# Graph attention over 400,000 sorted edges: the gathers of a pair of sections split into two groups of four, the first group turned half a step ahead

## The chip, the cores and the metric

The kernel runs on one core of a Trainium2 chip, as one launch. The metric is the device time of one execution in microseconds, and the figure for a kernel is the median over repeated executions. Beside the times there is one profiled execution with a trace of every engine: TensorE (PE, with its weight loads shown apart as PEld), VectorE (DVE), ScalarE (ACT), GpSimd (POOL) and SyncE (SP), which issues most of the plain transfers.

## The reference

One graph attention layer over 12,500 nodes of 128 channels and 400,000 edges, whose edges come sorted by their target node. Cut to what matters:

```python
h = relu(layernorm(x))
msg_src, msg_dst = h @ w_src + b_src, h @ w_dst
message = msg_src[src] + msg_dst[dst]                      # 400,000 x 128
rad_w = silu(silu(edge_attr_32 @ w1 + b1) @ w2 + b2) @ w3 + b3
message = (message * edge_weight1 * rad_w) @ w_sep + b_sep
msg_h = message.reshape(E, 8, 32)
alpha, value = smooth_leaky_relu(msg_h[..., :16]), msg_h[..., 16:]
score = einsum('ehk,ahk->eh', alpha, alpha_dot)
att = segment_softmax(score, dst)
out = segment_sum(value * att, dst).reshape(N, 128)
x = x + out @ w_proj + b_proj
```

## The kernel before

There are three stages. The first computes the two node tables (msg_src, msg_dst) and writes them to device memory. The second, the function `windows`, walks over the edges and takes nearly all of the time. The third divides, projects and adds x.

In `windows` a **tile** is T = 125 edges, a **section** is four tiles (500 edges), and a **pair** is two sections (1000 edges). There are NP = 400 pairs and one `step(k)` per pair (L939). Tensors lie with channels on the 128 partitions and the section's 500 edges along the row, so that one bank of PSUM holds one section. The instructions of each engine run in exactly the order in which `step` calls the helpers; nothing reorders them later. An instruction waits on semaphores for its operands and for the buffer it writes.

The pair k passes through several steps, since the helpers work on different pairs at once:

- `gather(k)` (L734), called in step k-4: eight indirect transfers on POOL's queue, one per tile, each of which brings 125 rows of the msg_src table (the rows that the edges' `src` names) into one slot of the tile `gs`. `gs` holds eight slots, and there are four such tiles in rotation, so the gathers of pair k+4 write into the tile of pair k.
- `e_T`, `mlp1`, `mlp2` (L745, L753, L765) in the steps k-3, k-2 and k-1: the edge attributes are turned, then go through the two hidden layers. `mlp1` multiplies on 64 of the 128 rows of the array, two halves side by side; `mlp2` uses all 128.
- `one_hot_T(k)` and `split_md(k, ...)` in step k-1: operands for the target rows' share of the message.
- `mlp3(k)` (L777) in step k: the third layer (half-height products into the two-bank tile `p3`); DVE makes `rad` from it, in two instructions, by adding a bias and multiplying by the edge weight.
- `message(k, rad)` (L791) in step k: eight **turnings** on PE (L796, matmuls by the identity that transpose a gathered tile into PSUM, four into each of the two `pm` banks); then six products of one-hot matrices (L802), which add the target rows in the same banks; then two DVE instructions (L807), which multiply `pm` by `rad` into `mT`, one per section.
- `alphas(k, f)` (L809) in step k, once per section f: a product into the one bank `pa`, ACT's silu, DVE's `al`, which also frees `pa`.
- `scores(k)` in odd steps, for two pairs. Every eight steps DVE scans the scores for the softmax (`softmax_up`, `softmax_down`, `softmax_exp`), and PE turns the result (`softmax_T`).
- `values(c, f)` (L887) and `sums(c)` (L899) with c = k-12: four products into the one bank `V`, DVE's `pvx` (which frees `V`), then sixteen products that sum a window of nodes.

The part of `step` that sets PE's order in a steady step, in words: mlp3(k), the eight turnings of pair k, the six one-hot products, values(c, 0), alphas(k, 0), values(c, 1), mlp1(k+2), mlp2(k+1), alphas(k, 1), sums(c), e_T(k+3), in odd steps scores(k), then mlp3(k+1). DVE's order is: rad twice, mT twice, pvx of section 0, a small subtraction (L728), al of section 0, pvx of section 1, the one-hot of k+1 (L774), L732, al of section 1, any scan, then two comparisons (L879, L882) for the next step, then the next rad.

PSUM's eight banks are all taken: `misc`, `m1`, `p3` (two), `pm` (two), `pa` and `V`.

Of the kernel before, what the change touches and what calls it, by code (L numbers as in the profile page):

```python
# [21 lines left out]
F32 = mybir.dt.float32  # L22
# [8 lines left out]
P = 128  # L31
C = 128
# [13 lines left out]
T = 125  # L46
TS = 4
SEC = T * TS
# [8 lines left out]
def gnn_kernel(ctx: ExitStack, tc: tile.TileContext, a: dict, out: bass.AP):  # L57
    nc = tc.nc
# [46 lines left out]
    ident = const.tile([P, P], F32, name="ident")  # L105
# [550 lines left out]
    def windows():  # L656
# [5 lines left out]
        with tc.tile_pool(name="wk2", bufs=2) as sp, tc.tile_pool(name="ps", bufs=1, space=PSUM) as pp, \  # L662
                tc.manual_schedule(), ExitStack() as held:
            lp = held.enter_context(tc.tile_pool(name="ld", bufs=2))
            prep, e_g, d_g, w_g, md, gath = {}, {}, {}, {}, {}, {}
            eTs, h1s, h2s, ohT, m3, mr, mTs, als, S_all, sms, Ps, Pem, pvx, ohs, accs, xs, Ms = (
                {} for _ in range(17))


            def prep_load(u):  # L670
# [60 lines left out]
                else:  # L731
                    nc.vector.tensor_sub(m3[k][:, 2, :], mr.pop(k), m3[k][:, 1, :])  # L732

            def gather(k):  # L734
                gs = lp.tile([P, 8, C], F32, name="gs", bufs=4)
                idx, _ = prep[k // 16]
                for j in range(8):
                    t = k % 16 * 8 + j
                    nc.gpsimd.indirect_dma_start(  # L739
                        out=gs[:, j, :], out_offset=None, in_=t_src[:, :],  # L740
                        in_offset=bass.IndirectOffsetOnAxis(ap=idx[:, t:t + 1], axis=0))
                gath[k] = gs


            def e_T(k):  # L745
# [31 lines left out]
            def mlp3(k):  # L777
                p3 = pp.tile([C, 2, BANK], F32, name="p3")
                for f in range(2):
                    s = slice(f * FC, (f + 1) * FC)  # L780
                    nc.tensor.matmul(p3[:, f, 0:SEC], w3b[s, :], h2s[k][s, :], start=True, stop=True)  # L781
                rad = sp.tile([C, PR], F32, name="rad", bufs=1)
                v = "x (t h p) -> x h t p"
                n = dict(t=4, h=2)
                for h in range(2):
                    nc.vector.scalar_tensor_tensor(  # L786
                        rad.rearrange(v, **n)[:, h], p3[:, h, 0:SEC].rearrange("x (t p) -> x t p", t=4),
                        b3, w_g[k].rearrange(v, **n)[:, h], op0=ALU.add, op1=ALU.mult)
                return rad

            def message(k, rad):  # L791
                gs = gath[k]
                pm = [pp.tile([C, SEC], F32, name="pm", bufs=2) for _ in range(2)]
                for f in range(2):
                    for t in range(TS):
                        nc.tensor.matmul(pm[f][:, t * T:(t + 1) * T], gs[:T, f * TS + t, :],  # L796
                                         ident[:T, :T], start=(t == 0), stop=False,
                                         is_transpose=True, skip_group_check=True)
                for j in range(3):
                    for f in range(2):  # L800
                        s = slice(f * W, (f + 1) * W)
                        nc.tensor.matmul(pm[f], m3[k][s, j, :], ohT[k][s, :], start=False, stop=(j == 2),  # L802
                                         skip_group_check=True)
                mTs[k] = sp.tile([C, PR], F32, name="mT", bufs=LAG + 1)
                for f in range(2):
                    s = slice(f * SEC, (f + 1) * SEC)
                    nc.vector.scalar_tensor_tensor(mTs[k][:, s], pm[f], b_n, rad[:, s], op0=ALU.add, op1=ALU.mult)  # L807
# [63 lines left out]
            def sums_begin(c):  # L871
                pvx[c] = sp.tile([T, 2, TS, ROW], F32, name="pvx")
                q = c % MP * 2
                for f in range(2):
                    nc.scalar.copy(pvx[c][:, f, :, C:ROW], Pem[c // MP][:, :, q + f, :])
                _, loc = prep[c // 16]
                ohs[c] = sp.tile([T, 8, W], F32, name="oh")
                t0 = c % 16 * 8
                nc.vector.tensor_tensor(  # L879
                    ohs[c][:, :, 0:W - 1], lane[:T, 0:W - 1].unsqueeze(1).to_broadcast([T, 8, W - 1]),  # L880
                    loc[:, t0:t0 + 8].unsqueeze(2).to_broadcast([T, 8, W - 1]), op=ALU.is_equal)
                nc.vector.tensor_tensor(  # L882
                    ohs[c][:, :, W - 1].rearrange("p (f t) -> p f t", f=2),
                    loc[:, t0:t0 + 8].rearrange("p (f t) -> p f t", f=2),
                    far[:T, 2 * c:2 * c + 2].unsqueeze(2).to_broadcast([T, 2, TS]), op=ALU.is_equal)

            def values(c, f):  # L887
                V = pp.tile([T, TS, C], F32, name="V") if c < NP - LAG else \
                    pp.tile([T, TS, C], F32, name="pm", bufs=2)
                for t in range(TS):  # L890
                    o = f * SEC + t * T
                    nc.tensor.matmul(V[:, t, :], mTs[c][:, o:o + T], w_v, start=True, stop=True)  # L892
                q = c % MP * 2 + f
                nc.vector.tensor_mul(  # L894
                    pvx[c][:, f, :, 0:C].rearrange("p t (h k) -> p t h k", h=H),
                    V.rearrange("p t (h k) -> p t h k", h=H),
                    Pem[c // MP][:, :, q, :].unsqueeze(3).to_broadcast([T, TS, H, C // H]))
# [12 lines left out]
            def store_win(c):  # L910
                nc.sync.dma_start(out=win[c * P:(c + 1) * P, :], in_=accs[c])
# [20 lines left out]
            def has(k):  # L932
                return 0 <= k < NP
# [5 lines left out]
            def step(k):  # L939
                c = k - LAG  # L940
                if has(c - 1):
                    store_win(c - 1)
                    store(c - 1, 0)

                if k % 16 == 4 and has(k + 12):
                    prep_load((k + 12) // 16)
                if has(k + 3):
                    load_w(k + 3)
                    load_md(k + 3)
                if k % 2 and has(k + 3):  # L950
                    load_d((k + 3) // 2)
                if has(k + 6) and k >= -4:
                    load_e(k + 6)
                if has(k + 4) and (k + 4) % MP == 0:
                    load_sm((k + 4) // MP)
                if has(c - 1):
                    store(c - 1, 1)
                if 0 <= 2 * k < NZ:
                    for i in range(2 * k, min(2 * k + 2, NZ)):
                        zero(i)  # L960
                if k % 16 == 8 and has(k + 8):
                    prep_make((k + 8) // 16)
                i, q = divmod(k - 40, MP)
                if 0 <= i < Q and q == 5:
                    load_x(i)
                if 0 <= i < Q and q == 7:
                    add_x(i)
                if has(k + 4):
                    gather(k + 4)
                if has(k + 1):  # L970
                    split_md(k + 1, 0)
                if has(c):
                    sums_begin(c)
                if has(k):
                    message(k, mlp3(k))
                if has(c):
                    values(c, 0)
                if has(k + 1):
                    split_md(k + 1, 1)
                if has(k):  # L980
                    alphas(k, 0)
                if has(k + 1):
                    split_md(k + 1, 2)
                if has(c):
                    values(c, 1)
                if has(k + 2):
                    mlp1(k + 2)
                if has(k + 1):
                    mlp2(k + 1)
                    one_hot_T(k + 1)  # L990
                    split_md(k + 1, 3)
                if has(k):
                    alphas(k, 1)
                if has(c):
                    sums(c)
                m, r = divmod(k, MP)
                if has(k - MP):
                    if r == 1:
                        softmax_up(m - 1)
                    elif r == 2:  # L1000
                        softmax_down(m - 1)
                        softmax_exp(m - 1)
                    elif r == 3:
                        softmax_T(m - 1)
                if has(k + 3):
                    e_T(k + 3)
                if has(k) and k % 2 == 1:
                    scores(k)

            for k in range(-5, NP):  # L1010
                step(k)
# [156 lines left out]
    with tc.If(unfit == 0) as fit:  # L1168
        windows()
# [26 lines left out]
    with tc.tile_pool(name="fin", bufs=3) as fp, tc.tile_pool(name="fin1", bufs=1) as f1, \  # L1196
# [7 lines left out]
        gs, qs, qTs, has = {}, {}, {}, {}  # L1204
# [104 lines left out]
```

## Time and profile before

| | us |
|---|---|
| median of 14 runs | 4761.37 |
| lowest and highest of them | 4757.42, 4764.04 |
| the profiled execution's own time | 4759.45 |
| its span in the trace | 4757.6 |
| granted TensorE clock, mean over the span | 0.976 of full |
| busy: PE, PEld | 4370.4, 2420.2 |
| busy: DVE, ACT, POOL | 3135.5, 1982.3, 3122.5 |

A row of the groups reads: the line of the kernel, the engine, the operation, what is written from what, how many; then the busy time, the mean duration of one in ns, and the idle time of the engine just ahead of these instructions with the event that ended most of it. A line of the timeline reads: start and duration in us, engine, line, operation, tiles, how many; the idle time before in square brackets, with its releaser. For PE the ends of matmuls are modelled, so the durations of neighbouring PE lines overlap a little; the starts are what is compared in this document.

### The profile page before, as it was taken

The numbers are of one execution on the slowest core, as the hardware profiler recorded it, in microseconds if no ns is written. First come the engines' busy times: TensorE is split into PE (matmuls) and PEld (weight loads), VectorE is DVE, ScalarE is ACT, GpSimd is POOL, SyncE is SP. The second block draws the span as 40 slices with busy tenths as digits, with TensorE's granted clock in tenths as the row PEclk, the third lists the DMA queues.
The fourth block names the chain that finished last, engine by engine and source line by source line (L and its number), as shares of the span: only waits on it lengthen the run. The fifth ranks groups of instructions, "written<-read, shape, count | busy, mean of one in ns | idle before, by whom it ended". The sixth has DMA issues, their size and how long they took to land.

```text
span 4757.6 us, 83248 instructions
## 1 busy us (share of the span) xinstructions
PE 4370.4 (92%) x27292; PEld 2420.2 (51%) x27292; DVE 3135.5 (66%) x6006; ACT 1982.3 (42%) x4595; POOL 3122.5 (66%) x3223
## 2 busy tenths in 40 slices
PE   4779999999999999999999999999999999999974
PEld 3325555555555555555555555555555555555554
DVE  4446666666666666666666666666666666666666
ACT  4324444444444444444444444444444444444421
POOL 0567767777777777777776776776777777777701
PEclk8889999999999999999999999999999999999986
DMA  4667777777777777777777777676767777676624
GB/s 163 168 166 174 170 172 176 167 175 178 165 178 171 171 178 170 176 174 167 178 173 169 179 168 168 169 164 169 171 160 168 173 161 169 166 168 169 163 57 171
DMA packets 901130, 796.02 MB, mean 167 GB/s; under 512 B 529965, under 2 KB 776669, under 8 KB 900438
## 3 DMA queue, kind: packets, MB, share of 16 engines
q1 hardware_dynamic: 794670, 573.33, 46.1%
q0 software_dynamic: 102816, 210.37, 21.6%
q10 hardware_dynamic: 3202, 6.92, 0.4%
q8 instruction: 218, 3.57, 0.3%
q14 instruction: 224, 1.84, 0.1%
HBM read 649.96 MB, written 140.67 MB: 166 GB/s over the span
## 4 chain that ended last, share of the span: by engine, by line
PE 63%; DVE 19%; DMA 6%; SPq 4%; issue 4%; ACT 3%; POOL 1%; ACTq 0%; DVEq 0%; POOLq 0%
PE V L892 9%; PE m L767 8%; DVE mT L807 8%; PE misc L903 7%; PE pa L811 7%; PE p L781 7%; PE pm L796 6%; DVE pvx L894 6%; PE pm L802 5%; PE p L758 5%; PE misc L822 4%; DMA agg<-ob 2%; PE m L749 2%; DVE rad L786 1%; DVE M L848 1%
## 5 line engine op out<-in xcount | busy, mean ns | idle before, releaser
L739 POOL DMA_INDIRECT gs<-t_src,idx x3200 | 3108.1, 971 | 1409.2 <-issue 874.1
L815 DVE SCALAR_TENSOR_TENSOR al<-pa,sl 128x500 f32<-128x500 f32 x800 | 542.9, 679 | 926.5 <-ACT sl L813 888.9
L813 ACT ACTIVATE sl<-pa,c_b_a 128x500 f32<-128x500 f32 x800 | 542.0, 678 | 1414.2 <-PE pa L811 1413.4
L892 PEld LDWEIGHTS V<-c_w_v,mT 128*125 128x125 f32 x6208 | 735.6, 187 | 527.7 <-DVE pvx L894 366.9
L892 PE MATMUL V<-c_w_v,mT 128*125 128x128 f32 x6208 | 883.6, 285 | 53.4
L811 PE MATMUL pa<-mT,c_w_a 128*128 128x500 f32 x1600 | 830.6, 601 | 89.7 <-DVE mT L807 65.9
L786 DVE SCALAR_TENSOR_TENSOR rad<-p,c_fc_b,w_b 128x500 f32<-128x500 f32 x800 | 552.4, 732 | 318.8 <-PE p L781 318.8
L807 DVE SCALAR_TENSOR_TENSOR mT<-pm,c_b_n,rad 128x500 f32<-128x500 f32 x800 | 553.4, 733 | 129.2 <-PE pm L802 121.0
L894 DVE TENSOR_TENSOR pvx<-V,Pem 125x512 f32<-125x512 f32 x776 | 528.0, 680 | 0.0
L903 PEld LDWEIGHTS misc<-pvx,oh 125*64 125x64 f32 x6400 | 362.6, 137 | 323.6 <-ACT h L769 285.7
L903 PE MATMUL misc<-pvx,oh 125*64 125x136 f32 x6400 | 467.5, 287 | 32.4 <-DVE pvx L894 27.0
L796 PEld LDWEIGHTS pm<-ident,gs 125*128 125x128 f32 x3200 | 338.5, 141 | 302.3 <-issue 290.8
L781 PE MATMUL p<-h,w3b 64*128 64x500 f32 x1600 | 446.4, 635 | 0.0
L767 PE MATMUL m<-h,w2b 128*128 128x500 f32 x800 | 446.0, 640 | 0.0
L796 PE MATMUL pm<-ident,gs 125*128 125x125 f32 x3200 | 432.5, 278 | 3.5 <-DMA gs<-t_src,idx 3.5
L811 PEld LDWEIGHTS pa<-mT,c_w_a 128*128 128x128 f32 x1600 | 267.9, 190 | 305.5 <-issue 155.6
L761 ACT ACTIVATE h<-p,b 128x500 f32<-128x500 f32 x400 | 272.5, 681 | 352.0 <-PE p L758 344.7
L769 ACT ACTIVATE h<-m,b 128x500 f32<-128x500 f32 x400 | 270.9, 677 | 128.3 <-PE m L767 118.3
L802 PE MATMUL pm<-ohT,m 64*128 64x500 bf16 x2400 | 323.7, 376 | 0.0
L758 PE MATMUL p<-eT,w1b 64*128 64x250 f32 x1600 | 280.1, 427 | 1.0 <-ACT eT L751 1.0
L879 DVE TENSOR_TENSOR oh<-lane,loc 125x504 f32<-125x504 f32 x400 | 271.6, 679 | 0.0
L822 PE MATMUL misc<-al,w_s 128*32 128x500 f32 x1600 | 228.2, 601 | 25.1 <-ACT Pem L868 22.7
(146 smaller groups left out, 3144.7 us busy)
## 6 DMA issues: line engine op xcount, KB each, us to landing
w_b<-in_edge_weight SPq DMA_DIRECT2D x400, 500.0 KB
d_b<-in_dst SPq DMA_DIRECT2D x400, 250.0 KB
gs<-t_src,idx POOLq DMA_INDIRECT x3200
e_t<-in_edge_attr SPq DMA_DIRECT2D x400, 125.0 KB
sc_d<-Sp SPq DMA_DIRECT2D x200, 250.0 KB
win<-ob SPq DMA_DIRECT2D x400, 68.0 KB
agg<-ob SPq DMA_DIRECT2D x800, 33.5 KB
md<-t_dst SPq DMA_DIRECT2D x800, 32.0 KB
```

Source lines behind the costliest of these rows:

```text
L739: nc.gpsimd.indirect_dma_start(out=gs[:, j, :], out_offset=None, in_=t_src[:, :], in_offset=bass.IndirectOffsetOnAxis(ap=idx[:, t:t + 1], ...
L767: nc.tensor.matmul(p2, w2b, h1s.pop(k), start=True, stop=True)
L781: nc.tensor.matmul(p3[:, f, 0:SEC], w3b[s, :], h2s[k][s, :], start=True, stop=True)
L786: nc.vector.scalar_tensor_tensor(rad.rearrange(v, **n)[:, h], p3[:, h, 0:SEC].rearrange("x (t p) -> x t p", t=4), b3, w_g[k].rearrange(v, ...
L796: nc.tensor.matmul(pm[f][:, t * T:(t + 1) * T], gs[:T, f * TS + t, :], ident[:T, :T], start=(t == 0), stop=False, is_transpose=True, skip_ ...
L802: nc.tensor.matmul(pm[f], m3[k][s, j, :], ohT[k][s, :], start=False, stop=(j == 2), skip_group_check=True)
L807: nc.vector.scalar_tensor_tensor(mTs[k][:, s], pm[f], b_n, rad[:, s], op0=ALU.add, op1=ALU.mult)
L811: nc.tensor.matmul(pa, w_a, mTs[k][:, f * SEC:(f + 1) * SEC], start=True, stop=True)
L815: nc.vector.scalar_tensor_tensor(al, pa, 0.25, sl, op0=ALU.mult, op1=ALU.add)
L892: nc.tensor.matmul(V[:, t, :], mTs[c][:, o:o + T], w_v, start=True, stop=True)
L894: nc.vector.tensor_mul(pvx[c][:, f, :, 0:C].rearrange("p t (h k) -> p t h k", h=H), V.rearrange("p t (h k) -> p t h k", h=H), Pem[c // MP] ...
L903: nc.tensor.matmul(acc[f * W:(f + 1) * W, :], ohs[c][:, f * TS + t, :], pvx[c][:, f, t, :], start=(t == 0), stop=(t == TS - 1), skip_group ...
```

## The change

`gather(k)` and its tile are split in two: `gather(k, f)` fetches the four tiles of one section into a tile `gs0` or `gs1` of half the size, again with four of each in rotation. The four turnings of a section become a function of their own, `sources(k, f)`, which takes one PSUM bank for it (`pm0` or `pm1`, one bank each, where there was `pm` with two). `message` keeps the one-hot products and `mT`. The call of `sources(k, 1)` stands between `mlp3(k)` and the one-hot products; `sources(k+1, 0)` stands in the step before, between `mlp1(k+2)` and `mlp2(k+1)`. Each is followed by the gather that reuses its buffer: `gather(k+4, 1)` and `gather(k+5, 0)`.

```diff
-            def gather(k):
-                gs = lp.tile([P, 8, C], F32, name="gs", bufs=4)
+            def gather(k, f):
+                gs = lp.tile([P, TS, C], F32, name=f"gs{f}", bufs=4)
                 idx, _ = prep[k // 16]
-                for j in range(8):
-                    t = k % 16 * 8 + j
+                for j in range(TS):
+                    t = k % 16 * 8 + f * TS + j
...
-                gath[k] = gs
+                gath[k, f] = gs
...
+            def sources(k, f):
+
+                gs = gath.pop((k, f))
+                pms[k, f] = pp.tile([C, SEC], F32, name=f"pm{f}")
+                for t in range(TS):
+                    nc.tensor.matmul(pms[k, f][:, t * T:(t + 1) * T], gs[:T, t, :], ident[:T, :T],
+                                     start=(t == 0), stop=False, is_transpose=True, skip_group_check=True)
+
             def message(k, rad):
-                gs = gath[k]
-                pm = [pp.tile([C, SEC], F32, name="pm", bufs=2) for _ in range(2)]
-                for f in range(2):
-                    for t in range(TS):
-                        nc.tensor.matmul(pm[f][:, t * T:(t + 1) * T], gs[:T, f * TS + t, :],
-                                         ident[:T, :T], start=(t == 0), stop=False,
-                                         is_transpose=True, skip_group_check=True)
+                pm = [pms.pop((k, f)) for f in range(2)]
...
                 V = pp.tile([T, TS, C], F32, name="V") if c < NP - LAG else \
-                    pp.tile([T, TS, C], F32, name="pm", bufs=2)
+                    pp.tile([T, TS, C], F32, name=f"pm{f}")
...
-                if has(k + 4):
-                    gather(k + 4)
                 if has(k + 1):
                     split_md(k + 1, 0)
                 if has(c):
                     sums_begin(c)
+                rad = mlp3(k) if has(k) else None
                 if has(k):
-                    message(k, mlp3(k))
+                    sources(k, 1)
+                if has(k + 4):
+                    gather(k + 4, 1)
+                if has(k):
+                    message(k, rad)
...
                 if has(k + 2):
                     mlp1(k + 2)
+
+                if has(k + 1):
+                    sources(k + 1, 0)
+                if has(k + 5):
+                    gather(k + 5, 0)
                 if has(k + 1):
                     mlp2(k + 1)
```

More of the change, by code (lines that the diff above doesn't have):

```diff
@@ L665, in windows @@
             prep, e_g, d_g, w_g, md, gath = {}, {}, {}, {}, {}, {}
-            eTs, h1s, h2s, ohT, m3, mr, mTs, als, S_all, sms, Ps, Pem, pvx, ohs, accs, xs, Ms = (
-                {} for _ in range(17))
+            eTs, h1s, h2s, ohT, m3, mr, mTs, als, S_all, sms, Ps, Pem, pvx, ohs, accs, xs, Ms, pms = (
+                {} for _ in range(18))
             def prep_load(u):
```

## The prediction

> **What bounds the kernel now.** I read the page's busy times first, then the groups, then the timeline of two neighbouring steps.
>
> ```profile
> PE 4370.4 (92%) x27292; PEld 2420.2 (51%) x27292; DVE 3135.5 (66%) x6006; ACT 1982.3 (42%) x4595; POOL 3122.5 (66%) x3223
> ...
> L739 POOL DMA_INDIRECT gs<-t_src,idx x3200 | 3108.1, 971 | 1409.2 <-issue 874.1
> ...
> L892 PEld LDWEIGHTS V<-c_w_v,mT 128*125 128x125 f32 x6208 | 735.6, 187 | 527.7 <-DVE pvx L894 366.9
> L892 PE MATMUL V<-c_w_v,mT 128*125 128x128 f32 x6208 | 883.6, 285 | 53.4
> ```
>
> PE is the busy engine. But the weight loads of V (L892) sat behind DVE's pvx for 366.9 us in 388 places (the waits list them), about once per pair that has values, while the matmul row shows only 53.4 us of idle time. Which row is true is settled by starts. This is a steady odd step; its mlp3 starts at 2130.70, and I write times from there ("+4.92").
>
> ```profile
> 2130.70 1.11 PE L781 MATMUL p<-h,w3b 64*128 64x500 f32 x4
> 2131.74 1.07 PE L796 MATMUL pm<-ident,gs 125*128 125x125 f32 x8
> 2131.86 1.38 DVE L786 SCALAR_TENSOR_TENSOR rad<-p,c_fc_b,w_b 128x500 f32<-128x500 f32 x2 [0.34 <-PE p L781]
> 2132.74 0.81 PE L802 MATMUL pm<-ohT,m 64*128 64x500 bf16 x6
> 2133.48 1.14 PE L892 MATMUL V<-c_w_v,mT 128*125 128x128 f32 x8
> 2133.58 1.38 DVE L807 SCALAR_TENSOR_TENSOR mT<-pm,c_b_n,rad 128x500 f32<-128x500 f32 x2 [0.34 <-PE pm L802]
> 2134.45 1.02 PE L811 MATMUL pa<-mT,c_w_a 128*128 128x500 f32 x2
> 2134.88 0.68 DVE L894 TENSOR_TENSOR pvx<-V,Pem 125x512 f32<-125x512 f32 x1
> 2135.62 1.14 PE L892 MATMUL V<-c_w_v,mT 128*125 128x128 f32 x8
> 2136.69 0.69 PE L758 MATMUL p<-eT,w1b 64*128 64x250 f32 x4
> 2137.31 1.11 PE L767 MATMUL m<-h,w2b 128*128 128x500 f32 x2
> 2138.25 1.00 PE L811 MATMUL pa<-mT,c_w_a 128*128 128x500 f32 x2
> 2139.18 0.89 PEld L903 LDWEIGHTS misc<-pvx,oh 125*64 125x64 f32 x16 [0.74 <-ACT h L769]
> ```
>
> The reader is to see two halves. **First half, mlp3 to the second V:** PE does mlp3 (+0), turnings (+1.04), one-hot products (+2.04), V (+2.78), pa (+3.75), and starts the second V at +4.92. The second pa of the step takes 0.93 from its start to the sums (2138.25 to 2139.18); so the first would have let V start at +4.68. It starts 0.06 after the pvx that began at 2134.88 and took 0.68. V has one bank, so PE waits 0.24 for DVE. DVE's part is a chain: rad, rad, mT, mT, pvx, with one hole of 0.34 ahead of mT, ended by the one-hot products. **Second half, the second V to the next mlp3:** each PE line starts where the one before it ends; PE alone sets it. Steady even steps take 9.93 us and odd ones 11.05 (the starts of L781), the difference being scores.
>
> POOL issues a gather each 0.94 us with 0.30 between, (3108.1+874.1)/400 = 9.96 us a pair, against a mean of (4550.06-330.13)/387 = 10.90 us per step from the 13th mlp3 to the last. Its remaining idle time is mostly waiting for turnings to free a buffer: it is ahead by all four pairs, and PE waited for gathers 3.5 us in all.
>
> **The change part by part.**
>
> *The turnings that leave the first half.* Four of eight go. The eight take 1.00 (2131.74 to 2132.74), four so 0.50. The one-hot products start at +1.54 and V at +2.28. But DVE's rad still starts at +1.16, when mlp3 has its sums, and mT follows both rads. What that costs when PE is not what ends the wait is shown by the step after the next, where a scan delayed DVE:
>
> ```profile
> 2154.24 1.37 DVE L786 SCALAR_TENSOR_TENSOR rad<-p,c_fc_b,w_b 128x500 f32<-128x500 f32 x2
> 2155.72 1.38 DVE L807 SCALAR_TENSOR_TENSOR mT<-pm,c_b_n,rad 128x500 f32<-128x500 f32 x2
> 2156.51 1.10 PE L811 MATMUL pa<-mT,c_w_a 128*128 128x500 f32 x2 [0.91 <-DVE mT L807]
> 2157.02 0.68 DVE L894 TENSOR_TENSOR pvx<-V,Pem 125x512 f32<-125x512 f32 x1
> 2157.75 0.95 PEld L892 LDWEIGHTS V<-c_w_v,mT 128*125 128x125 f32 x8 [0.94 <-DVE pvx L894]
> ```
>
> From rad to mT 1.48, from mT to pa 0.79, from mT to the second V 2.03. So in the new steady step mT starts at 1.16+1.48 = +2.64 (was +2.88), pa at +3.43 (PE is there at 3.75-0.50 = +3.25 and waits 0.18), the second V at 2.64+2.03 = +4.67 (PE is there at 3.43+0.93 = +4.36 and waits 0.31). The half shrinks from 4.92 to 4.67: -0.25, half of the work taken out. The other half of it turns into waiting for DVE.
>
> *The turnings that enter the second half.* Four between mlp1 and mlp2, where PE has no hole: +0.50. Behind them in PE's queue are mlp2, the second pa, sums, e_T and the next mlp3, each of which comes 0.50 later after the second V. DVE's comparisons and so the next rad hang on the second pa and move with it. Nothing gives the 0.50 back.
>
> The steady step thus grows by 0.25. Three kinds of steps, with values in 388 steps:
> - 48 steps after a softmax_down (one in eight): rad starts at about +2.6 there, mT is already DVE's, and the second V does not move. +0.50, less 0.04 by which the second pa waits for al today: 0.46 x 48 = 22 us.
> - 24 steps in which DVE adds x ahead of the comparisons: rad starts at +1.38, the second V at 1.38+1.48+2.03 = +4.89. +0.47 x 24 = 11 us.
> - The 316 others: 0.25 x 316 = 79 us.
> - The first 12 steps have no V, and at a mean clock of 0.80 (180 to 325 us) PE's share is larger. Between -0.25 and twice 0.50 for each: -3 to +12 us. I take 0, since their 163 us also hold POOL's start.
>
> Sum: +112 us.
>
> *The new waits.* Each group of turnings waits for its four gathers, and the early group for `pm0`, which mT of the pair before freed before pa could run: no cost. The gathers are still asked for four pairs ahead. Had PE to wait for a gather, mlp2 and all behind it would stand; the 3.5 us of today bound that from above if the distance holds, and four pairs at over 10 us hold it. Bounds 0 to 4 us; I take 0.
>
> *POOL.* Two waits for PE per pair instead of one, each half a step apart. POOL needs 9.96 of a pair's 11.2 us, so a buffer that comes free earlier saves nothing on the path, and a second wait costs nothing until it takes over 1 us per pair. The same 3200 transfers of the same size; SP's queue is untouched.
>
> *The place.* The early group stands behind half-height products. mlp1's slot is 0.62 (2136.69 to 2137.31), although 250 columns at the pace of mlp2 (0.94 for 500) come to 0.47: 0.15 goes at such a change of shape. Today mlp1 is followed by mlp2, also a full-height product, so the number of changes stays; the added group costs 0.50 by its own row, or 0.65 if the new border adds such a 0.15: 388 x 0.15 = +58 us. I take the first, since its neighbour's shape is the nearest row. The Trainium skill, in "TensorEngine Tiling (Array Packing)", section Key Properties, says that changing the tiling mode drains the TensorE, and speaks against inserting there; by its words the number of drains is the same and the sum stays, and with one drain more at the estimate above it would be +170.
>
> A second rule bears on which row to believe. The skill's "Perfetto Trace Analysis", section Identifying the Most-Contended Engine, calls the matmul busy share a poor measure; here, 53.4 us idle against 527.7 at the weight loads of the same line. Taken from the matmul row alone, PE would be full, the change would only reorder its work, and the sum would be 0.
>
> On its own time the profiled execution goes from 4759.45 to 4871; the median lay 1.9 above it, so 4873 us.
>
> **The rivals.**
> - *It covers holes* (faster). If PE had 0.5 us of holes per step between the second V and the next mlp3, the turnings would fill them, and the first half's -0.25 would stand: 316 x -0.25 = -79, 4682 us. It decides from a hole of over 0.25 us per step. Against it: the starts in the second half, back to back in every steady step. For it: only that ends of matmuls are modelled. 4 in 100.
> - *Order does not matter* (same). If mT could start as soon as the one-hot products end (+2.38), the second V would come at +4.41, PE would lose no more than today: within 10 us of 4761. Against it: rad's two instructions, at 1.38 from +1.16. 6 in 100.
> - *The border costs more* (slower still): +58, 4931 us. 13 in 100.
> - *POOL or the clock becomes the bound.* POOL, if its second wait cost over 1 us; the clock, if the added waiting lowered the grant, which is 1.00 from 325 to 4555 us today, through holes of about 1 us. A grant of 0.5 as in the first steps would give thousands. 3 in 100.
>
> The forecast has the other 74, with its own range of 4840 to 4905: the mT wait may be 0.07 shorter (-22), the four turnings 0.48 (-8), the first steps +12, the rest +20.
>
> **How the numbers follow.** The range goes from 4825 to 4935: it takes in the border and a third of the way to "same". About 0.2% (10 us) is what a measurement can tell from no change. Faster: 4 in 100; within: 6; slower: 90.
>
> **What would show it.** Right: one-hot products 0.50 earlier from mlp3 and mT 0.24 earlier, rad directly followed by mT; a wait for mT ahead of the first pa in most steps, where today 60 steps have one; steps of about 10.2 and 11.3 us; mlp2 0.5 later after mlp1. Wrong: steps of 9.7 (holes), an unchanged 9.93, or mlp1 to mlp2 over 1.2 (the border); POOL without a wait for turnings would mean that it bounds.

## The result, and the profile after

The changed kernel takes 4820.03 us, the median of 6 runs (4817.12 to 4823.53), against 4760.67 for the kernel before on the same chip: a ratio of 1.0125, with a 95% interval of 1.0115 to 1.0135. It is slower by 59 us where 112 were forecast, and lies 5 us below the range. The profiled execution took 4823.72 us, 3.7 over the median, with a span of 4821.7, at the same mean granted clock as before, 0.976.

From the page, the busy times and those groups that answer to the ones shown of before:

```profile
PE 4413.7 (92%) x27292; PEld 2426.0 (50%) x27292; DVE 3102.4 (64%) x6006; ACT 1980.6 (41%) x4595; POOL 3055.3 (63%) x3223
...
L739 POOL DMA_INDIRECT gs<-t_src,idx x3200 | 3040.9, 950 | 1535.4 <-issue 778.8
...
L894 PEld LDWEIGHTS V<-c_w_v,mT 128*125 128x125 f32 x6208 | 735.8, 187 | 527.3 <-DVE pvx L896 365.8
L813 PE MATMUL pa<-mT,c_w_a 128*128 128x500 f32 x1600 | 852.3, 615 | 107.3 <-DVE mT L809 86.7
L894 PE MATMUL V<-c_w_v,mT 128*125 128x128 f32 x6208 | 883.8, 286 | 53.2
```

The groups hardly tell the two kernels apart. V's weight loads wait for pvx as long as before (365.8 against 366.9 us, some 0.95 per place): that is the idle time of the weight loads, and it does not tell how long PE itself waits. Only the timeline shows what happened. A steady odd step of the kernel after, whose mlp3 starts at 2119.02:

```profile
2119.02 1.11 PE L781 MATMUL p<-h,w3b 64*128 64x500 f32 x4
...
2120.06 0.65 PE L796 MATMUL pm<-ident,gs 125*128 125x125 f32 x4
2120.18 1.38 DVE L786 SCALAR_TENSOR_TENSOR rad<-p,c_fc_b,w_b 128x500 f32<-128x500 f32 x2 [0.43 <-PE p L781]
...
2120.64 0.81 PE L804 MATMUL pm<-ohT,m 64*128 64x500 bf16 x6
...
2121.37 1.14 PE L894 MATMUL V<-c_w_v,mT 128*125 128x128 f32 x8
...
2121.66 1.38 DVE L809 SCALAR_TENSOR_TENSOR mT<-pm,c_b_n,rad 128x500 f32<-128x500 f32 x2
...
2122.45 1.11 PE L813 MATMUL pa<-mT,c_w_a 128*128 128x500 f32 x2
...
2122.96 0.68 DVE L896 TENSOR_TENSOR pvx<-V,Pem 125x512 f32<-125x512 f32 x1
...
2123.70 1.14 PE L894 MATMUL V<-c_w_v,mT 128*125 128x128 f32 x8
...
2124.77 0.69 PE L758 MATMUL p<-eT,w1b 64*128 64x250 f32 x4
...
2125.39 0.41 PEld L796 LDWEIGHTS pm<-ident,gs 125*128 125x128 f32 x4 [0.32 <-issue]
2125.39 0.65 PE L796 MATMUL pm<-ident,gs 125*128 125x125 f32 x4
...
2125.77 0.30 PEld L767 LDWEIGHTS m<-h,w2b 128*128 128x128 f32 x2
2125.87 1.01 PE L767 MATMUL m<-h,w2b 128*128 128x500 f32 x2
...
2126.72 1.00 PE L813 MATMUL pa<-mT,c_w_a 128*128 128x500 f32 x2
```

Read the starts. rad runs straight into mT, whose hole of 0.34 is gone, and the second V stands at +4.68 (before +4.92). In the second half the early turnings start 0.62 after mlp1 and mlp2 another 0.48 later; but the pa behind mlp2 follows after 0.85, where it took 0.94 before.

Below, a **slot** is the time from the start of one PE group to the start of the next. The medians over all steady steps:

| | before | after |
|---|---|---|
| second V, from mlp3 | +4.92 | +4.68 |
| mlp1 (slot) | 0.62 | 0.62 |
| early turnings (slot) | - | 0.48 |
| mlp2 (slot) | 0.94 | 0.84 |
| second pa to the next mlp3, even steps | 2.37 | 2.37 |
| turnings behind mlp3 (slot) | 1.00, eight | 0.58, four |
| steady even step, odd step | 9.93, 11.05 | 10.07, 11.20 |
| step after a softmax_down | 13.73 | 13.86 |

Over the whole span of the two profiled executions: the 314 steady steps of the trace bring 46.3 us, the 48 after a softmax_down 7.4, the 25 with x (the prediction counted 24) 7.0, the first 12 steps 2.1, all before the first mlp3 2.6 and all after the last -1.3; together 64.1, the difference of the spans (4821.7 - 4757.6).

### The profile page after: what moved, and what is told of

It is laid out like the page before. It is cut to its first block, busy times and chain, and to the rows that moved or that the text cites. A ratio compares the mean times of both kernels' runs of the same rounds, so it can differ in the third digit from the quotient of the medians.

```text
span 4821.7 us, 83644 instructions
## 1 busy us (share of the span) xinstructions
PE 4413.7 (92%) x27292; PEld 2426.0 (50%) x27292; DVE 3102.4 (64%) x6006; ACT 1980.6 (41%) x4595; POOL 3055.3 (63%) x3223
## 4 chain that ended last, share of the span: by engine, by line
PE 51%; DVE 27%; DMA 6%; issue 6%; SPq 5%; ACT 3%; POOL 0%; DVEq 0%; ACTq 0%; POOLq 0%
DVE rad L786 9%; PE V L894 9%; PE pa L813 7%; PE misc L905 7%; DVE mT L809 6%; PE m L767 6%; PE p L781 6%; DVE pvx L896 5%; PE p L758 5%; PE pm L796 5%; PE misc L824 4%; DMA agg<-ob 2%; PE m L749 2%; SPq L917 1%; DVE oh L881 1%
## 5 line engine op out<-in xcount | busy, mean ns | idle before, releaser
L739 POOL DMA_INDIRECT gs<-t_src,idx x3200 | 3040.9, 950 | 1535.4 <-issue 778.8
L894 PEld LDWEIGHTS V<-c_w_v,mT 128*125 128x125 f32 x6208 | 735.8, 187 | 527.3 <-DVE pvx L896 365.8
L813 PE MATMUL pa<-mT,c_w_a 128*128 128x500 f32 x1600 | 852.3, 615 | 107.3 <-DVE mT L809 86.7
L796 PE MATMUL pm<-ident,gs 125*128 125x125 f32 x3200 | 522.8, 286 | 8.1 <-DMA gs<-t_src,idx 7.9
L813 PEld LDWEIGHTS pa<-mT,c_w_a 128*128 128x128 f32 x1600 | 272.3, 190 | 357.4 <-DVE mT L809 113.1
L767 PE MATMUL m<-h,w2b 128*128 128x500 f32 x800 | 404.9, 588 | 0.0
```

The costliest lines, as they stand in the source:

```text
L739: nc.gpsimd.indirect_dma_start(out=gs[:, j, :], out_offset=None, in_=t_src[:, :], in_offset=bass.IndirectOffsetOnAxis(ap=idx[:, t:t + 1], ...
L767: nc.tensor.matmul(p2, w2b, h1s.pop(k), start=True, stop=True)
L796: nc.tensor.matmul(pms[k, f][:, t * T:(t + 1) * T], gs[:T, t, :], ident[:T, :T], start=(t == 0), stop=False, is_transpose=True, skip_group ...
L813: nc.tensor.matmul(pa, w_a, mTs[k][:, f * SEC:(f + 1) * SEC], start=True, stop=True)
```

## The experiments

**Theory A** takes the steps above at their word: the first half gives 0.24, because DVE's chain rad, rad, mT, mT, pvx sets the second V; the group in the second half costs 0.48 and makes mlp2 0.10 cheaper, so +0.38. **Rival B**: the move costs the 112 us of the forecast, and the divided gathers, whose buffers come free earlier, give some 50 of them back.

A first series (e1_split_only, e2_move_only, e3_after_mlp2, e4_before_v1, then e4b_before_v1 and e5_one_rad_after) met chips on which even the kernel before took 6390 to 6512 us (at granted clocks of 0.87 to 0.88; the edited kernels had 0.84 to 0.93), so their totals say nothing of the edits, and five of the kernels were run again where the kernel before took 4760. Their totals, each against the kernel before beside it:

| | us | before | ratio |
|---|---|---|---|
| e1_split_only | 6848.7 | 6511.9 | 1.051 |
| e2_move_only | 6958.0 | 6511.9 | 1.068 |
| e3_after_mlp2 | 5947.5 | 6511.9 | 0.913 |
| e4_before_v1 | 6957.6 | 6511.9 | 1.068 |
| e4b_before_v1 | 6606.1 | 6403.6 | 1.034 |
| e5_one_rad_after | 5709.7 | 6389.8 | 0.887 |

What differed there is told under the hardware below.

**The division alone** (e1, e1b): the gathers in two groups, all turnings in their old place.

```diff
-                if has(k):
-                    sources(k, 1)
-                if has(k + 4):
-                    gather(k + 4, 1)
+                for f in range(2):
+                    if has(k):
+                        sources(k, f)
+                    if has(k + 4):
+                        gather(k + 4, f)
...
-                if has(k + 1):
-                    sources(k + 1, 0)
-                if has(k + 5):
-                    gather(k + 5, 0)
```

> Gathers and buffers are divided in two groups of four, but all eight turnings stay between mlp3 and the one-hot products, so PE's order is that of before. Theory A (borders: the moved turnings cost 0.38 us instead of 0.50, since mlp2 behind them is 0.11 shorter; the division of the gathers does nothing): 4761, within 6 us, steps of 9.93 and 11.05. Theory B (the moved turnings do cost 0.50, and the divided gathers give some 50 us back): about 4710, steps of 9.80 and 10.92.

Repeated:

> Gathers divided, all turnings in their old place, again. Theory A: 4760, within 6 us. Theory B (the division gives back 50 us): about 4710.

Measured: 4756.64 against 4760.75, ratio 0.9991 (0.9982 to 1.0001); steps of 9.93, 11.05 and 13.63. The division does nothing that can be told from no change, and B falls. Only the 48 steps after a softmax_down are shorter, by 0.08 in the mean (4 us together); the next run, with the gathers undivided and the turnings moved, has it too. What the two share is the function `sources` with its banks `pm0` and `pm1`; whether that is the reason was not tried.

**The move alone** (e2, e2b): one gather of eight into one tile, as before, but half of its turnings in the new place.

```diff
-            def gather(k, f):
-                gs = lp.tile([P, TS, C], F32, name=f"gs{f}", bufs=4)
+            def gather(k):
+                gs = lp.tile([P, 8, C], F32, name="gs", bufs=4)
...
-                    gather(k + 4, 1)
+                    gather(k + 4)
...
-                if has(k + 5):
-                    gather(k + 5, 0)
```

> One gather of eight per pair as before, freed by the second group of turnings, but the first group of turnings stands half a step ahead as in the changed kernel. Theory A: 4820, within 6 us, steps of 10.07 and 11.20. Theory B: 4873, steps of 10.18 and 11.30.

Repeated:

> One gather of eight, the first group of turnings moved half a step ahead, again. Theory A: 4820, within 6 us. Theory B: 4873.

Measured: 4821.91 against 4760.75, ratio 1.0129 (1.0112 to 1.0145); steps of 10.07, 11.20 and 13.86, as in the kernel after. The slower time is the move of four turnings.

**Another neighbour for the group** (e3, e3b): the block `sources(k+1, 0)`, `gather(k+5, 0)` between mlp2 and the second pa, both products on all 128 rows.

```diff
-                if has(k + 1):
-                    sources(k + 1, 0)
-                if has(k + 5):
-                    gather(k + 5, 0)
                 if has(k + 1):
                     mlp2(k + 1)
                     one_hot_T(k + 1)
                     split_md(k + 1, 3)
+                if has(k + 1):
+                    sources(k + 1, 0)
+                if has(k + 5):
+                    gather(k + 5, 0)
```

> The changed kernel with the early group one place later, between mlp2 and the second pa, both full-height products. Theory A: mlp2's slot goes back from 0.84 to 0.95, the four turnings cost about 0.105 each there (slope of the slots: 0.58 for four, 1.00 for eight), the step is 10.07 + 0.11 + 0.42 - 0.49 = 10.11, 4835 us. If a group of four costs 0.50 wherever it stands (the prediction's row): 10.18, about 4863. If the place does not matter: 4820.

Repeated:

> The early group between mlp2 and the second pa, again. Theory A: the group costs 0.43 there and mlp2 0.94, together 0.05 more than the changed kernel's 0.48 and 0.84: steps of 10.12 and 11.25, about 4838 us. If the place does not matter: 4820. If four turnings cost 0.50: 4863.

Measured: 4840.56 against 4760.75, ratio 1.0172 (1.0155 to 1.0189); steps of 10.12 and 11.25. From its timeline:

```profile
2508.00 0.30 PEld L767 LDWEIGHTS m<-h,w2b 128*128 128x128 f32 x2 [0.32 <-issue]
2508.00 1.10 PE L767 MATMUL m<-h,w2b 128*128 128x500 f32 x2
...
2508.95 0.59 PE L796 MATMUL pm<-ident,gs 125*128 125x125 f32 x4
...
2509.37 1.01 PE L813 MATMUL pa<-mT,c_w_a 128*128 128x500 f32 x2
```

mlp2, behind mlp1 again, has its 0.94 back, and its weight load starts together with it (2508.00 both), not ahead; the group between two full-height products costs only 0.43 (the median; 0.42 in this step). So it is the neighbour that decides: 0.94 + 0.43 here, 0.48 + 0.84 in the kernel after, 0.05 per step less, which in 388 steps is 19 us; 20.5 were measured between the two (4840.56 - 4820.03).

**The group doubled** (e7): the early four turnings are done twice.

```diff
-                for t in range(TS):
+                for t in [*range(TS)] * (2 - f):
```

> The changed kernel with the early group of turnings done twice over (the second time over the first, so that the output is the same). Theory A: a further four cost 4 x 0.105 = 0.42 us a step with no border of their own, the slot from the group to mlp2 grows from 0.48 to 0.90 and mlp2 stays at 0.84: 4820 + 168 = 4988. By the prediction's price of 0.125 each: 5020.

Measured: 4985.15 against 4759.55, ratio 1.0480 (1.0462 to 1.0497); steps of 10.50 and 11.63, 0.43 more than the kernel after. Its timeline:

```profile
2499.93 0.69 PE L758 MATMUL p<-eT,w1b 64*128 64x250 f32 x4
...
2500.56 1.07 PE L796 MATMUL pm<-ident,gs 125*128 125x125 f32 x8
...
2501.47 1.01 PE L767 MATMUL m<-h,w2b 128*128 128x500 f32 x2
...
2502.31 1.00 PE L813 MATMUL pa<-mT,c_w_a 128*128 128x500 f32 x2
```

The group of eight takes 0.91 and mlp2 0.84 again. The slope is (0.91 - 0.48)/4 = 0.107 per turning, not the 0.125 that a row of eight taking 1.00 gives on average.

**One rad** (e5, e5b on the kernel after; e6 on the kernel before): if DVE's chain holds the second V, half of rad must bring the kernel after the other part of its gain, and the kernel before nothing in a steady step. Both use the first section's rad for both sections and leave the second half of the radial weights out.

```diff
-                rad = sp.tile([C, PR], F32, name="rad", bufs=1)
...
-                for h in range(2):
-                    nc.vector.scalar_tensor_tensor(
-                        rad.rearrange(v, **n)[:, h], p3[:, h, 0:SEC].rearrange("x (t p) -> x t p", t=4),
-                        b3, w_g[k].rearrange(v, **n)[:, h], op0=ALU.add, op1=ALU.mult)
+                rad = sp.tile([C, SEC], F32, name="rad", bufs=1)
+                nc.vector.scalar_tensor_tensor(rad, p3[:, 0, 0:SEC], b3, w_g[k][:, 0:SEC],
+                                               op0=ALU.add, op1=ALU.mult)
...
-                    nc.vector.scalar_tensor_tensor(mTs[k][:, s], pm[f], b_n, rad[:, s], op0=ALU.add, op1=ALU.mult)
+                    nc.vector.scalar_tensor_tensor(mTs[k][:, s], pm[f], b_n, rad, op0=ALU.add, op1=ALU.mult)
```

> The changed kernel with rad made for one of the two halves only and used for both sections (the other half of the radial weights is left out, so the messages are not the reference's). Theory A: DVE's chain loses one instruction of 0.65 us and mT is then released by the one-hot products at about +2.45 instead of +2.65; PE reaches pa and the second V 0.2 earlier, and the steady step falls from 10.07 to about 9.87, 4745 us. If PE's queue alone set the step: no change, 4820.

Repeated:

> The changed kernel with rad made for one of the two halves only and used for both sections (the second half of the radial weights is left out). Theory A: one DVE instruction of 0.65 us leaves the chain, mT is released by the one-hot products at 1.62 + 0.84 = +2.46 instead of +2.65, the second V comes at about +4.49 instead of +4.68, the steady step falls from 10.07 to 9.88, and by some 0.65 in the 48 steps after a softmax_down: 4820 - 65 - 31 = 4724. If PE's queue alone set the steady step: only the 48 steps gain, 4790.

> The kernel before with the same cut of rad. Theory A: the one-hot products release mT there, not rad, so the steady steps stay 9.93 and 11.05 and only the 48 steps after a softmax_down gain 0.65: about 4730, so that the gap of 59 us between the two orders closes to nothing. If the gap came from anything but DVE's chain in the first half, it stays about 59.

Measured: on the kernel after 4723.94, ratio 0.9926 (0.9909 to 0.9943) to 4759.55, steps of 9.89, 11.01 and 13.23; on the kernel before 4731.17, ratio 0.9938 (0.9922 to 0.9955), its steady steps unchanged at 9.93 and 11.06, the one after a softmax_down at 13.09. With one rad the move is 7 us faster instead of 59 slower. DVE in the kernel after with one rad (mlp3 at 2507.79):

```profile
2508.95 0.74 DVE L783 SCALAR_TENSOR_TENSOR rad<-p,c_fc_b,w_b 128x500 f32<-128x500 f32 x1 [0.43 <-PE p L781]
2510.25 1.38 DVE L805 SCALAR_TENSOR_TENSOR mT<-pm,c_b_n,rad 128x500 f32<-128x500 f32 x2 [0.56 <-PE pm L800]
2511.55 0.68 DVE L892 TENSOR_TENSOR pvx<-V,Pem 125x512 f32<-125x512 f32 x1
```

mT is released by the one-hot products again, at +2.46 instead of +2.64, and the second V comes at +4.50.

**The group where PE waits** (e4, e4b, e4c): the block between the first pa and the second V.

```diff
+                if has(k + 1):
+                    sources(k + 1, 0)
+                if has(k + 5):
+                    gather(k + 5, 0)
                 if has(c):
                     values(c, 1)
                 if has(k + 2):
                     mlp1(k + 2)
-                if has(k + 1):
-                    sources(k + 1, 0)
-                if has(k + 5):
-                    gather(k + 5, 0)
```

> The changed kernel with the early group between the first pa and the second V, where PE waits for DVE's pvx. Theory A (PE loses in the first half what it waits for the chain rad, rad, mT, mT, pvx): PE reaches the second V at 3.44 + 0.93 + 0.42 = +4.79 and pvx is done at +4.68, so the step is 9.93 - 4.92 + 4.79 = 9.80 in 340 steps, and unchanged in the 48 after a softmax_down: 4717 us. If PE's own sum of work were the limit and the order did not matter: 4761, as before. If the turnings were dear for being divided, wherever they stand: about 4820.

Repeated, twice:

> The same kernel as e4_before_v1, again, since in that series the kernel before itself took 6512 us. Theory A: 4717 against 4761 for the kernel before, steps of about 9.80 and 10.92, pa at +3.44 and the second V at +4.79 after mlp3. If order does not matter: 4761. If divided turnings are dear anywhere: 4820.

> The early group between the first pa and the second V, a third time, in a series in which the kernel before took its usual 4759 us. From the slots seen in the first two series (the group 0.43, the second V behind it 0.97 instead of 1.07): steady steps of 3.44 + 0.94 + 0.43 = +4.81 to the second V, then 0.97 and the old rest, 9.72 and 10.85; theory A 4680 to 4717. If PE is full and order does not matter: 4761. If divided turnings are dear anywhere: 4820.

Measured: 4711.09 against 4760.75, ratio 0.9894 (0.9878 to 0.9911), faster than both kernels; steps of 9.72, 10.85 and 13.63. V's rows of its page, and the place in its timeline:

```profile
L894 PE MATMUL V<-c_w_v,mT 128*125 128x128 f32 x6208 | 847.6, 279 | 0.1
L894 PEld LDWEIGHTS V<-c_w_v,mT 128*125 128x125 f32 x6208 | 739.7, 188 | 161.7 <-issue 160.4
```

```profile
2502.73 1.10 PE L813 MATMUL pa<-mT,c_w_a 128*128 128x500 f32 x2
2503.24 0.68 DVE L896 TENSOR_TENSOR pvx<-V,Pem 125x512 f32<-125x512 f32 x1
...
2503.67 0.59 PE L796 MATMUL pm<-ident,gs 125*128 125x125 f32 x4
...
2504.10 1.04 PE L894 MATMUL V<-c_w_v,mT 128*125 128x128 f32 x8
...
2505.07 0.69 PE L758 MATMUL p<-eT,w1b 64*128 64x250 f32 x4
```

The wait for pvx is gone from V's rows (365.8 us in the kernel after), the group of 0.43 fills it, and the second V itself takes 0.97 instead of 1.07. The kernel as it was changed thus put the four turnings where PE had no hole, two groups behind the place where it waits.

**The same hole, other work** (e8, on the kernel before): e_T(k+3), a slot of 0.36 us behind the sums in even steps, between the first pa and the second V.

```diff
+                if has(k + 3):
+                    e_T(k + 3)
                 if has(c):
                     values(c, 1)
...
-                if has(k + 3):
-                    e_T(k + 3)
```

> The kernel before, with all eight turnings in their old place, and e_T (two turnings of edge attributes, a slot of 0.36 to 0.44 us) moved from behind the sums to the place between the first pa and the second V. Theory A (PE waits 0.24 us there for DVE's pvx in every steady step): the move fills the wait, PE reaches the second V at about 4.68 + 0.36 = +5.04 instead of +4.92, the slot of the second V shrinks from 1.07 to 0.97 since its weights are loaded ahead, and the step falls from 9.93 to about 9.6 to 9.7: 4640 to 4680 against 4761. If PE is full and order does not matter: 4761.

Measured: 4744.94 against 4759.45, ratio 0.9970 (0.9958 to 0.9981): faster, but far less than expected. Even steps fell from 9.93 to 9.56, the whole e_T, a little more than expected. Odd steps stayed at 11.05, and those after a softmax_down grew by 0.9. An even step, whose mlp3 starts at 2117.40:

```profile
2121.16 1.03 PE L811 MATMUL pa<-mT,c_w_a 128*128 128x500 f32 x2
...
2121.59 0.68 DVE L894 TENSOR_TENSOR pvx<-V,Pem 125x512 f32<-125x512 f32 x1
...
2122.02 0.38 PE L749 MATMUL m<-ident,e_t 125*128 125x125 f32 x2
...
2122.32 1.14 PE L892 MATMUL V<-c_w_v,mT 128*125 128x128 f32 x8
```

The second V still starts at +4.92, 0.05 behind pvx, so e_T fits into the hole whole. It also sizes the hole: the first pa, at +3.76, takes 0.86 up to e_T, so that PE waits 0.30 in the kernel before and not the 0.24 that the prediction took from the second pa, whose 0.93 ends at the sums. In an odd step:

```profile
2114.83 1.15 PE L903 MATMUL misc<-pvx,oh 125*64 125x136 f32 x16
2116.35 1.12 PE L822 MATMUL misc<-al,w_s 128*32 128x500 f32 x8 [0.37 <-ACT ob L907]
```

Here e_T had covered ACT's copy of the sums out of `misc`, the bank that scores writes. The 0.37 that it left became a wait of 0.37. In the steps after a softmax_down mlp2 comes 1.36 behind mlp1 instead of 0.62: it writes the bank `m1` that e_T wrote, and waits there for ACT's copy of e_T (L751), by 0.67 in every one of the 48. That is most of the 0.9; why the first pa comes 0.32 later in these steps stays open.

**Both** (e9): e4 with e_T(k+3) between the first V and the first pa in even steps, where no scores wait.

```diff
+                if has(k + 3) and k % 2 == 0:
+                    e_T(k + 3)
                 if has(k):
                     alphas(k, 0)
...
-                if has(k + 3):
+                if has(k + 3) and k % 2 == 1:
                     e_T(k + 3)
```

> The early group between the first pa and the second V, and e_T in even steps between the first V and the first pa, where PE still waits about 0.11 for mT. Theory A: the even steps fall from 9.72 to about 9.61, odd ones stay 10.85: 4711 - 22 = 4690. If that wait is not real: 4711.

Measured: 4686.36 (4678.51 to 4696.85) against 4759.55, ratio 0.9842 (0.9825 to 0.9858): the fastest version. The total is the expected one by two misses of opposite sign. Even steps fell by 0.36 (expected 0.11). One of them, whose mlp3 starts at 2396.26:

```profile
2399.59 0.38 PE L749 MATMUL m<-ident,e_t 125*128 125x125 f32 x2
2399.81 1.00 PE L813 MATMUL pa<-mT,c_w_a 128*128 128x500 f32 x2
2400.65 0.59 PE L796 MATMUL pm<-ident,gs 125*128 125x125 f32 x4
```

pa starts at +3.55 (+3.44 in e4c), but behind e_T it takes 0.84 where it took 0.94 and no longer waits, so the turnings stand at +4.39 as against +4.38, and e_T costs nothing there. But the steps after a softmax_down grew from a mean of 13.64 to 14.23 and those four steps later by 0.38. Four of eight steps by -0.36 and these two make (-1.44 + 0.59 + 0.38)/8 = -0.06 per step, 23 us; 24.7 were measured to e4c. (The steps are those of the profiled run, which was the slowest of the four.) What e_T covered in the two longer steps was not tried.

## Why the prediction was right or wrong

- *First half*: right. The second V was put at +4.67 and stands at +4.68; mT at +2.64 and is at +2.65; rad runs straight into mT, and e5b shows that DVE's chain owns the wait. The work taken out was put too high here as well, without effect on V, which DVE sets: the one-hot products come 0.43 earlier (+1.62) and not 0.50 (+1.54). Of the 0.43, 0.24 were gained and 0.19 turned into waiting, where the prediction had 0.25 and 0.25: the first pa comes 0.11 later than PE could be there (+3.44; +3.33 in e5b), and its slot is 0.94 after that wait (e4c) where it is 0.86 without one (e8). The hole ahead of the second V stays at 0.30. One sign was not there as described: the waits of PE list hardly more places at the first pa than before (67 against 60). The wait is there (the slot from the first V to pa has a median of 1.08 where a V without a wait behind it takes 0.97), but shows in part at pa's weight loads, which wait for mT 113.1 us in 110 places (81.7 in 60 before), and mostly in no list at all.
- *Second half*: **the step that failed is "Four between mlp1 and mlp2, where PE has no hole: +0.50", with "Nothing gives the 0.50 back".** mlp2 came 0.48 later after mlp1, almost as put; but mlp2's own slot fell from 0.94 to 0.84, so +0.38. Two things were in the wrong place. The 0.50 is half of a row of eight that took 1.00; by the slope of e7, eight turnings are 0.86 and the other 0.14 belongs to the row's two borders with half-height products, which stayed with the four that did not move (their slot is 0.58, not 0.50). And the border between mlp1 and mlp2, for which mlp2 paid 0.10, passed to the turnings, which pay 0.05 for it. So four at 0.107 are 0.43, the border makes them 0.48, and mlp2's 0.10 goes: 0.38. The prediction had said that the number of borders stays, and bounded the place from 0 to +0.15; it never bounded it from below nothing, by asking what the neighbour that loses the border would gain. The rule on drains that it quotes says only that a change of mode drains, and neither advises against inserting nor names who pays; here inserting made this border cheaper, 0.05 instead of 0.10. The term is 0.12 too large (0.116 before rounding), which in 388 steps is some 45 of the 53 us by which the forecast was off.

That mlp2's weights are not loaded ahead could be read before, but not what this costs. From the timeline of the kernel before, the weight loads that belong to the lines shown in the prediction:

```profile
2136.69 0.30 PEld L758 LDWEIGHTS p<-eT,w1b 64*128 64x128 f32 x4
...
2137.31 0.30 PEld L767 LDWEIGHTS m<-h,w2b 128*128 128x128 f32 x2 [0.32 <-issue]
...
2137.84 0.19 PEld L811 LDWEIGHTS pa<-mT,c_w_a 128*128 128x128 f32 x1 [0.23 <-issue]
```

mlp2's load starts at 2137.31, with its matmul; in the kernel after it starts at 2125.77, 0.10 ahead of the matmul at 2125.87. The load of the second pa, a product of the same shape, starts 0.41 ahead of its matmul at 2138.25, and yet its slot, which ends at the sums, is 0.93: a comparison of the two would have priced the difference at nothing. The Trainium skill, in "TensorE: Matmul & The Clock Gate", Part 2, section Step-by-step: what each phase is for, says that PE pulls a weight load ahead of matmuls in flight where the row groups don't conflict or the load goes to the background buffer. Behind full-height products the trace agrees; that the load is not ahead behind a half-height product is what the trace adds, and the page gives no price for it.

- *Steps after a softmax_down*: predicted +0.46, measured 0.15, for 48 steps 7.4 instead of 22 us. 0.12 of this is the term above. Besides, the second V came at +6.04 instead of +6.13, as DVE's chain behind the scan became a little shorter (it did so in e1b, where no turning moved), and the second pa, which had waited for al (+8.81), now comes too late to wait (+9.06), so that the sums follow it after 0.93 instead of 1.04. The term "less 0.04" was too small.
- *Steps with x*: +0.28 instead of +0.47 in 25 steps, 7.0 instead of 11 us; the same 0.12 and a rest of 0.07: rad starts there at +1.30 and not at +1.38 as in the kernel before, and so the second V at +4.82 and not at +4.89.
- *First steps, new waits, POOL, clock*: nearly within the bounds. The first 12 steps +2.1; PE waited for gathers 7.9 us in all (3.5 before), 0.4 more than the bound of 4, but all of it before 235 us, in those first steps and ahead of them; POOL waits for turnings 550.7 us (336.3 before) without a sign of an effect (in e1b it waits 423.5 and the time stays); the clock is the same.
- *The rivals*: "covers holes" and "order does not matter" did not come. "The border costs more" had the right place and the wrong sign. The range's lower end, called a third of the way to "same" (4825 is 48 of these 112 us from the forecast, over two fifths), was made from a rival and not from a bound of the term that was least known.

## What to carry to other kernels

Price a group of matmuls that moves by its slope and by its borders, on both sides of its old and its new place: look whether its neighbours' weights are loaded ahead of their matmuls, and let the neighbour's change of price have either sign. Put moved work where the engine waits, which the starts of neighbouring groups show and the idle time of matmul rows does not: four turnings cost 59 us between mlp1 and mlp2 and gave 50 just ahead of the V that waits. And ask what the work had been covering where it stood: e_T was worth 0.36 in even steps and nothing in odd ones.

## What the runs showed of the hardware

- A PE slot depends on its neighbours in steps of about 0.05 to 0.1 us. Four fp32 turnings take 0.58 between half-height products, 0.48 from half to full height and 0.43 between full-height ones. mlp2, a full-height product in two instructions of 500 columns, takes 0.84 behind turnings and 0.94 behind half-height products. pa, of the same shape, takes 0.84 to 0.86 between full-height neighbours (e9, e8), 0.94 after a wait for DVE (e4c) and 0.93 ahead of the sums. The second V takes 1.07 after a wait for DVE and 0.97 behind turnings (e4c).
- In the first series, where the kernel before took 6390 us and more, ACT came late behind PE: from the start of mlp2's second matmul to ACT's silu a median of 0.62 us passed in the profile of the kernel before (taken where it needs 4760), and 4.5 in that of e1_split_only. What brings this about stays open.
